# Three hand-written orders of one two-layer kernel, written anew

## The chip, the cores and the metric

One core of a Trainium2 chip runs the whole program. The metric is the device time of one execution in microseconds (us). It is measured on the chip, and several runs are taken. A profile of one execution comes with it: the start and duration of the instructions of each engine, what an engine waited for, and when the transfers landed. PE is the matrix engine, DVE the vector engine, ACT the scalar engine. POOL and SP issue transfers here and do little else.

## The reference

The input `x` is 16 images of 128 channels by 64 by 64 pixels, in float32. Two layers follow each other, both added to their input:

```python
# layer 0
v   = round(clip(gn(x) * input_factor, -1, 1) * 127) / 127 * 0.6     # group norm, then 8 bits
fv  = patches(v) + 0.1 * patches(v) ** 3                             # 3x3, padded by one
outs = [einsum('bctfyx,ocyx->btfo', fv, (g_pos - g_neg)[i]) for i in range(3)]
adc  = lambda y: clip(round(y * 0.01 * 256) / 256, -16, 16)
x = x + (adc(outs[2]) + 4*adc(outs[0]) + 2*adc(outs[1]) + 1*adc(outs[2])) * output_factor + bias
# layer 1
h  = gn(x)
q, k, v = Wq h, Wk h, Wv h
x  = x + Wm (q * (exp(B) (exp(k) * v)) / (exp(B) exp(k)))
```

`gn` is a group norm over 32 groups of 4 channels with all pixels of an image. So layer 0 is three 3x3 convolutions of 128 to 128 channels per image (one for each slice of the weights), and layer 1 is a chain of small matrix products for each pixel.

## The kernel before, in words

**The work.** A 3x3 convolution is done by a transform in both directions (rows by four, columns by two), so that it needs fewer products: an image's convolution with one weight slice (a *block*, 0, 1 or 2) has two halves, numbered `k` = 0 to 5 over the three blocks. Each product is 128x128 by 512 columns in float32. Layer 1 works on an image in four chunks, each a *pair* (numbers 0 to 3) of 1024 pixels.

**The operations.** Every step is a small function with a name, and three strings give the order in which the functions are called. The order in which they are called is the order of the instructions on every engine, because the schedule is manual. Each engine works through its own instructions strictly in this order; semaphores between engines are put in by the framework, where one operation needs another. Names that matter here:

- `q10.k q11.k q20.k ... q31.k`: PE, the products of half `k`, for two columns of the transform (last digit 0 or 1 before the dot). `q1u` starts a sum in a PSUM bank, `q2u` and `q0u` add to it, `q3u` adds to another bank.
- `m1u.k` (ACT, after `q1u`, before `q2u`), `sdu.k` (ACT, after `q2u`, before `q0u` and `q3u`), `sAu.k` (ACT, after `q0u`, before the next half's `q1u`): copies of the bank between the products. So PE needs ACT between any two of them.
- `Bo.k df.k sm.k` (DVE; `sm` of an even half is an adding transfer issued by POOL), `S0 S3 ma mc` (DVE): the back transform.
- `P.k`, `bc.k`, `o0.k o1.k`, `tk.k`: PE's product shared by two columns, DVE's spreading of it, eight more products of PE on the same bank, and ACT's taking of the bank. `bA bB` (DVE) bound the values, `aA aB` add them to the accumulator: for blocks 1 and 2 by an adding transfer on POOL's queue.
- `cx0..cx3` (ACT) turn the finished accumulator into four chunks; they need the last adding transfer `aB.1`. `cd0x..cd3x` (POOL) add the input to them by a transfer; `sq0..sq3` (ACT) sum squares; `ya pmy yb pvy yc yl yd` is the group norm between the layers (DVE, PE and ACT by turns).
- `xn kp vp qp ek ekv dn g u ln ex oa ob oc op r rd st` with a pair's number: layer 1. `xn ek g ln ex r` are ACT's, `kp vp qp dn op` PE's, `ekv u oa ob oc` DVE's, `rd` a transfer on POOL's queue and `st` a store on SP's.
- `li lj` (SP) load a chunk of the next image twice; `sx sy` (ACT) sum it and its squares, `x0 xa pmx xb pvx xc xl xd` is its group norm, `n` (ACT), `cl` (DVE), `s` (ACT), `va` (DVE) make the 8-bit values and their cubes, `gr er pa pb cs cq cd p0 p5 e0 e5` (DVE) the forward transform, `cp` (ACT) a copy.
- At the beginning only: `hs` (DVE, sum of a chunk), `hq` (ACT, its squares), `hn hc hr hv` as `n cl s va`, `hz hcs hcq hcd` (DVE, transform), and `W0a` to `W2p`: `Wia` negates weight slice `i` (ACT), `WiA` adds the positive weights to it by a transfer on POOL's queue, the other letters transform the weights (`c d e f h i k l o p` on DVE, `b g j J m n` on ACT).

**The lists.** `ORDER` is called for images 2 to 14 (13 times); an entry `q10.3+1` belongs to the turn before, so that the end of one image lies among the beginning of the next. `FIRST` is the work ahead of that: the weights and images 0 and 1. `LAST` is all that comes after, to the last store. Before the lists run, the four chunks of image 0 are loaded: 0 and 2 on SP's queue, 1 and 3 on ACT's. The lists are read by

```python
    for p in range(2, B - 1):
        turns[p] = operations(p)
        for e, s in order:
            o = turns[p - s].pop(e, None)
            if o is not None:
                o()
```

Of the kernel before, what the change touches and what calls it, by code (L numbers as in the profile page):

```python
# [70 lines left out]
    sA0.0+1 pmx+1 W2h+2 q31.0+1 q11.1+1 m11.1+1 xb+1 cq1+2 q10.1+1 W1l+2 m10.1+1 q21.1+1 lj1+1
    Bo.0+1 W2J+2 pvx+1 W2j+2 q20.1+1 sd0.1+1 q00.1+1 sd1.1+1 q01.1+1 W1k+2 q30.1+1 df.0+1 xc+1
    W1m+2 q31.1+1 p0+1 xl+1 W1o+2 W1n+2 xd+1 sA0.1+1 e0+1 n1+1 P.2+1 sm.0+1 q10.2+1 W1p+2 W2i+2
    Bo.1+1 W2l+2 n0+1 sA1.1+1 df.1+1 q11.2+1 m10.2+1 q20.2+1 sd0.2+1 cl0+1 q00.2+1 sm.1+1
    m11.2+1 ma.2+1 q21.2+1 sA0.2+1 sd1.2+1 q10.3+1 mc.2+1 q01.2+1 p5+1 s0+1 cl1+1 S0.2+1
    q30.2+1 q31.2+1 va0+1 s1+1 S3.2+1 sA1.2+1 lj3+1 W2m+2 q11.3+1 W2n+2 m10.3+1 Bo.2+1 bc.2+1
    m11.3+1 q20.3+1 bA.2+1 va1+1 df.2+1 q21.3+1 lj2+1 e5+1 sd0.3+1 sd1.3+1 n3+1 o1.2+1 n2+1
    o0.2+1 q00.3+1 gr0+1 q30.3+1 q31.3+1 sA0.3+1 q01.3+1 tk.2+1 P.3+1 W2p+2 li0+0 er0+1 sA1.3+1
    W2o+2 q10.4+1 Bo.3+1 sm.2+1 cp+1 bc.3+1 df.3+1 q11.4+1 m11.4+1 o0.3+1 cl2+1 cl3+1 W2k+2
    sx0+0 sm.3+1 s2+1 va2+1 mc.4+1 ma.4+1 q21.4+1 m10.4+1 q20.4+1 sd0.4+1 o1.3+1 sd1.4+1 S0.4+1  # L80
    aA.2+1 x0+0 q30.4+1 li1+0 tk.3+1 S3.4+1 q00.4+1 sA0.4+1 q31.4+1 P.4+1 bc.4+1 s3+1 q01.4+1
    q10.5+1 Bo.4+1 o1.4+1 bB.3+1 va3+1 sx1+0 bA.4+1 er1+1 m10.5+1 q20.5+1 sA1.4+1 aA.4+1 sy1+0
    q11.5+1 m11.5+1 o0.4+1 gr1+1 sd0.5+1 li3+0 tk.4+1 sy0+0 q21.5+1 P.5+1 q00.5+1 sd1.5+1
    q01.5+1 df.4+1 pb0+1 sA1.5+1 q30.5+1 sA0.5+1 q31.5+1 bc.5+1 pa0+1 o1.5+1 Bo.5+1 cq0+1
    df.5+1 cs0+1 o0.5+1 li2+0 tk.5+1 P.0+0 q10.0+0 sm.4+1 m10.0+0 q11.0+0 m11.0+0 sm.5+1
    q20.0+0 sd0.0+0 q21.0+0 sd1.0+0 cd0+1 q01.0+0 mc.0+0 aB.3+1 S0.0+0 bB.5+1 bc.0+0 sx2+0
    pa1+1 ma.0+0 pb1+1 q00.0+0 sA0.0+0 q30.0+0 o0.0+0 S3.0+0 o1.0+0 sy2+0 q31.0+0 aB.5+1 cs1+1
    sx3+0 sy3+0 bA.0+0 aA.0+0 tk.0+0 P.1+0 sA1.0+0 q11.1+0 q10.1+0 m10.1+0 lj1+0 bc.1+0 o0.1+0
# [9 lines left out]
    lj3+2 q31.2+2 S3.2+2 cl1+2 sA1.2+2 P.2+2 bc.2+2 q10.3+2 m10.3+2 q11.3+2 s1+2 cl0+2 Bo.2+2  # L98
    q20.3+2 bA.2+2 o0.2+2 m11.3+2 s0+2 sd0.3+2 sq1+2 va1+2 q21.3+2 sd1.3+2 lj2+2 o1.2+2 q30.3+2
    st3+2 sq2+2 q00.3+2 va0+2 sq3+2 q01.3+2 q31.3+2 df.2+2 gr0+2 tk.2+2 P.3+2 ya+2 pmy+2  # L100
    sA0.3+2 q10.4+2 er0+2 sA1.3+2 q11.4+2 yb+2 pvy+2 bc.3+2 Bo.3+2 n3+2 o1.3+2 cp+2 yc+2
    m10.4+2 n2+2 df.3+2 yl+2 st2+2 m11.4+2 yd+2 o0.3+2 xn0+2 cl2+2 cl3+2 sm.2+2 sm.3+2 mc.4+2
    s3+2 q20.4+2 kp0+2 vp0+2 ma.4+2 S0.4+2 tk.3+2 q21.4+2 P.4+2 sd0.4+2 q00.4+2 ek0+2 s2+2
    ekv0+2 dn0+2 sA0.4+2 va2+2 bB.3+2 sd1.4+2 g0+2 bc.4+2 u0+2 xn1+2 q10.5+2 oa0+2 q30.4+2
    o1.4+2 ln0+2 ex0+2 aA.2+2 o0.4+2 tk.4+2 q01.4+2 kp1+2 va3+2 qp0+2 ob0+2 bA.4+2 vp1+2 ek1+2
    gr1+2 oc0+2 op0+2 aB.3+2 q31.4+2 er1+2 sA1.4+2 ekv1+2 S3.4+2 Bo.4+2 q11.5+2 r0+2 P.5+2
    bc.5+2 dn1+2 df.4+2 pa0+2 m10.5+2 pb0+2 q20.5+2 m11.5+2 q21.5+2 sd0.5+2 g1+2 sd1.5+2 o1.5+2
    oa1+2 u1+2 o0.5+2 rd0+2 cs0+2 q00.5+2 ln1+2 ex1+2 sA0.5+2 tk.5+2 q30.5+2 cd0+2 q01.5+2
    q31.5+2 ob1+2 cq0+2 st0+2 bB.5+2 xn2+1 q10.0+1 qp1+2 oc1+2 sA1.5+2 kp2+1 vp2+1 m10.0+1
    ek2+1 op1+2 Bo.5+2 df.5+2 ekv2+1 q11.0+1 r1+2 m11.0+1 q20.0+1 aA.4+2 sm.5+2 dn2+1 sm.4+2  # L110
    mc.0+1 sd0.0+1 g2+1 S0.0+1 aB.5+2 q21.0+1 sd1.0+1 P.0+1 bc.0+1 u2+1 pa1+2 oa2+1 ln2+1 ex2+1
    ma.0+1 q00.0+1 rd1+2 q01.0+1 st1+2 ob2+1 S3.0+1 pb1+2 xn3+1 o1.0+1 o0.0+1 tk.0+1 q30.0+1
    kp3+1 qp2+1 vp3+1 oc2+1 op2+1 q31.0+1 cs1+2 ek3+1 ekv3+1 sA1.0+1 cq1+2 q11.1+1 Bo.0+1 r2+1
    P.1+1 bc.1+1 dn3+1 rd2+1 sA0.0+1 df.0+1 bA.0+1 g3+1 q10.1+1 sm.0+1 o0.1+1 u3+1 m10.1+1
    oa3+1 cd1+2 m11.1+1 o1.1+1 ln3+1 q21.1+1 tk.1+1 q20.1+1 bB.1+1 ex3+1 aA.0+1 sd0.1+1 sd1.1+1
    qp3+1 q00.1+1 sA0.1+1 ob3+1 oc3+1 q01.1+1 sA1.1+1 op3+1 r3+1 q10.2+1 aB.1+1 rd3+1 q30.1+1
    p0+1 m10.2+1 q31.1+1 e0+1 cx0+1 cd0x+1 q20.2+1 q11.2+1 cx1+1 cx2+1 p5+1 Bo.1+1 sd0.2+1
    P.2+1 df.1+1 y0+1 cd1x+1 m11.2+1 q21.2+1 sm.1+1 cd2x+1 cx3+1 mc.2+1 S0.2+1 sd1.2+1 q00.2+1
    q30.2+1 sA0.2+1 q01.2+1 ma.2+1 sA1.2+1 q10.3+1 bc.2+1 S3.2+1 e5+1 q11.3+1 q31.2+1 cd3x+1
    bA.2+1 o0.2+1 Bo.2+1 st2+1 st3+1 sq0+1 sq1+1 m10.3+1 m11.3+1 q20.3+1 df.2+1 sq2+1 q21.3+1  # L120
    sd0.3+1 sd1.3+1 o1.2+1 q30.3+1 sq3+1 q00.3+1 q31.3+1 ya+1 pmy+1 tk.2+1 P.3+1 yb+1 sA0.3+1
# [850 lines left out]
```

## Time and profile before

| What | us |
|---|---|
| median of 3 runs | 1596.8 (1596.6 to 1596.85) |
| span of the profiled execution, first to last instruction | 1594.6 |
| so outside the span, by the median | 2.2 |
| PE busy | 1488.2 |
| DVE busy | 1476.9 |
| ACT busy | 1184.6 |
| the first convolution product on PE | 46.6 |
| product `q10.3` in the first turn of ORDER, start | 156.74 |
| the same product in the 13th turn, start | 1287.74 |
| so one turn, the mean of the 12 between | 94.25 |

A line of the profile such as `L557 PE MATMUL` names the line of the kernel: L557 are all convolution products, L580, L582 and L585 ACT's copies `m1`, `sd` and `sA`, L588, L589 and L626 DVE's `Bo`, `df` and `bc`, L634 is `tk`, L644 `aB` and `aA`, L705 `cx`, L451 `n`, L365 all sums of squares, L434 `hs`, L318 the weights' `c`. One product of the convolution is two instructions, so `x2` on PE is one product. In a row of the timeline the first number is the start, the second the time covered, and what stands in brackets at the end is the idle time of the engine just before and what ended it.

### The profile page before, as it was taken

What the parts mean: (1) busy time and instruction counts of PE and PEld (TensorE: products, weight loads), DVE (VectorE), ACT (ScalarE), POOL (GpSimd) and SP (SyncE); (2) the same over time, 40 slices, a digit from 0 to 9 for tenths busy, and PEclk for the clock granted to TensorE, in tenths of its full rate; (3) what the DMA queues carried; (4) which work ended last, traced back from release to release, by engine and by line L of the source; (5) the groups of instructions that cost most, each with busy time, mean ns of one, the idle gap of its engine ahead of it and who ended that gap; (6) DMA issues with size and microseconds to landing.
All of it is one profiled execution on the core that took longest, in us unless ns stands there. A gap on an engine that the chain in (4) does not pass through costs nothing.

```text
span 1594.6 us, 14947 instructions
## 1 busy us (share of the span) xinstructions
PE 1488.2 (93%) x4684; PEld 564.8 (35%) x4684; DVE 1476.9 (93%) x1915; ACT 1184.6 (74%) x1859; POOL 227.8 (14%) x254
## 2 busy tenths in 40 slices
...
GB/s 184 81 92 119 104 160 173 124 206 111 148 130 166 184 119 191 125 136 144 149 208 115 154 130 151 163 134 197 117 149 133 157 183 119 202 62 123 76 128 149
DMA packets 67361, 227.03 MB, mean 142 GB/s; under 512 B 7632, under 2 KB 8272, under 8 KB 67280
## 3 DMA queue, kind: packets, MB, share of 16 engines
...
## 4 chain that ended last, share of the span: by engine, by line
PE 54%; issue 14%; DMA 13%; DVE 12%; ACT 5%; POOL 2%; DVEq 0%; POOLq 0%; ACTq 0%; SPq 0%
PE py L557 18%; PE pa L557 17%; PE pz L756 5%; PE pb L557 5%; DMA x<-in_x_dram 4%; PE pz L766 3%; DMA s<-s 3%; PE py L756 3%; DMA acc<-y 3%; PE py L778 2%; ACT x L705 2%; DVE acc L611 1%; DMA gmat<-in_x_dram 1%; DVE y L611 1%; DVE s L616 1%
## 5 line engine op out<-in xcount | busy, mean ns | idle before, releaser
L557 PE MATMUL py<-v,ud 128*128 128x512 f32 x760 | 357.5, 608 | 0.5
L557 PE MATMUL pa<-cs,us 128*128 128x512 f32 x384 | 199.2, 621 | 40.1 <-DVE cs L515 31.5
L557 PE MATMUL pa<-cd,us 128*128 128x512 f32 x384 | 202.8, 619 | 12.1 <-ACT pb L582 12.1
L557 PE MATMUL pa<-cq,us 128*128 128x512 f32 x384 | 198.5, 613 | 14.3 <-ACT d L580 14.2
L557 PEld LDWEIGHTS py<-v,ud 128*128 128x128 f32 x760 | 138.9, 189 | 182.0 <-issue 148.4
L557 PE MATMUL pb<-cd,us 128*128 128x512 f32 x384 | 194.3, 602 | 2.0 <-ACT pb L582 1.9
L580 ACT ACTIVATE d<-pa 128x512 f32<-128x512 f32 x192 | 112.1, 594 | 36.3 <-PE pa L557 20.4
L585 ACT ACTIVATE s<-pa 128x512 f32<-128x512 f32 x192 | 110.6, 591 | 35.3 <-PE pa L557 33.3
L582 ACT ACTIVATE pb<-pa 128x512 f32<-128x512 f32 x192 | 112.5, 586 | 29.7 <-PE pa L557 29.0
L819 POOL DMA_DIRECT2D xn<-x x58 | 58.3, 1010 | 521.1 <-ACT xn L789 520.8
L644 POOL DMA_DIRECT2D acc<-y x62 | 68.8, 1109 | 392.2 <-DVE y L637 243.7
L588 DVE SCALAR_TENSOR_TENSOR s<-d,pb 128x1024 f32<-128x1024 f32 x96 | 116.9, 1218 | 2.4 <-PE pb L557 2.0
L756 PE MATMUL pz<-xn,w 128*64 128x512 f32 x464 | 117.7, 607 | 0.6 <-ACT xn L803 0.6
L589 DVE TENSOR_TENSOR d<-s 128x1024 f32<-128x1024 f32 x96 | 117.3, 1221 | 0.4
L557 PEld LDWEIGHTS pa<-cs,us 128*128 128x128 f32 x384 | 66.0, 191 | 137.7 <-issue 64.4
L634 ACT ACTIVATE y<-py 128x1024 int16<-128x1024 f32 x62 | 82.6, 1333 | 41.4 <-PE py L557 40.2
L789 ACT ACTIVATE xn<-py,scalars 128x512 f32<-128x512 f32 x116 | 73.5, 685 | 51.1 <-PE py L778 51.1
L557 PEld LDWEIGHTS pa<-cq,us 128*128 128x128 f32 x384 | 68.0, 190 | 121.6 <-issue 71.9
L557 PEld LDWEIGHTS pa<-cd,us 128*128 128x128 f32 x384 | 66.8, 190 | 125.0 <-ACT pb L582 57.1
L557 PEld LDWEIGHTS pb<-cd,us 128*128 128x128 f32 x384 | 70.3, 190 | 96.4 <-issue 85.6
L557 PE MATMUL py<-sv,ud 128*128 128x512 f32 x192 | 98.6, 596 | 4.0 <-ACT y L634 1.9
L597 POOL DMA_DIRECT2D s<-s x48 | 45.3, 945 | 332.8 <-ACT gs L365 119.8
...
## 6 DMA issues: line engine op xcount, KB each, us to landing
xc<-in_x_dram SPq DMA_DIRECT2D x121, 512.0 KB, 5.4
...
```

The costliest lines, as they stand in the source:

```text
L557: pe.matmul(o if len(r.shape) == 2 else o.rearrange("p (t w) -> p t w", w=W2), w, r, start=start, stop=stop, skip_group_check=True,)
L580: f"m1{u}.{k}": lambda u=u, a=a: act.activation(d[:, u], a, AF.Copy),
L582: f"sd{u}.{k}": lambda a=a, b=b: act.activation(b, a, AF.Copy, scale=-1.0),
L585: f"sA{u}.{k}": lambda u=u, a=a: act.activation(s[:, u, 0], a, AF.Copy),
L588: f"Bo.{k}": lambda: dve.scalar_tensor_tensor(s[:, :, 1], d, 2.0, pb, ALU.mult, ALU.add),
L589: f"df.{k}": lambda: dve.tensor_tensor(d, s[:, 1], s[:, 0], ALU.subtract),
L634: act.activation(self.column(self.part(1)[0], h), y, AF.Copy)
L644: pool.dma_start(a, y, accum_op=ALU.add)
L756: pe.matmul(self.tiles(o)[h * IC : (h + 1) * IC], w, x[:, t[0] : t[1] : t[2]], start=True, stop=True)
L766: pe.matmul(o[c, t], eb[r, c], self.half(x)[r, t], start=True, stop=True, skip_group_check=True)
L789: act.activation(g[:, t], self.tiles(self.op[h]), AF.Identity, bias=bias_sb)
L819: "rd": lambda: pool.dma_start(self.r, self.x2, accum_op=ALU.add),
```

## The change

The three strings are replaced. No function differs, and every operation is called as often as before, for the same images. In `ORDER` each of the 307 entries is there again; six of them change the turn that they are counted to, since the cut between two turns lies elsewhere by a few entries (`P.2 q31.2 sA1.2` now on one side, `cd3x q30.2 sq0` on the other). `FIRST` has the same 409 entries and `LAST` the same 570, but for those six. The whole of `ORDER`, the beginning of `FIRST`, and the last image's end in `LAST`:

```diff
 ORDER = """
-    S3.2+1 cl1+1 q31.2+1 q10.3+1 cl0+1 P.2+1 sA1.2+1 q11.3+1 m10.3+1 bc.2+1 q20.3+1 o1.2+1 s1+1
-    m11.3+1 s0+1 Bo.2+1 sd0.3+1 sq1+1 va1+1 lj3+1 q21.3+1 o0.2+1 va0+1 sd1.3+1 q30.3+1 sq2+1
-    q00.3+1 q01.3+1 tk.2+1 lj2+1 sq3+1 df.2+1 er0+1 sA1.3+1 gr0+1 sA0.3+1 n3+1 P.3+1 ya+1 q31.3+1
-    bc.3+1 pmy+1 yb+1 n2+1 q11.4+1 st2+1 sm.2+1 q10.4+1 pvy+1 m10.4+1 o1.3+1 o0.3+1 Bo.3+1 yc+1
-    m11.4+1 df.3+1 yl+1 cp+1 yd+1 xn0+1 tk.3+1 ma.4+1 sm.3+1 q20.4+1 cl3+1 kp0+1 vp0+1 ek0+1
-    q21.4+1 mc.4+1 st3+1 cl2+1 sd0.4+1 bA.2+1 s3+1 S0.4+1 P.4+1 li0 xn1+1 s2+1 sd1.4+1 ekv0+1
-    bc.4+1 va3+1 q00.4+1 va2+1 dn0+1 g0+1 o0.4+1 o1.4+1 li1 q01.4+1 u0+1 ln0+1 oa0+1 tk.4+1 q30.4+1
-    S3.4+1 kp1+1 gr1+1 qp0+1 vp1+1 ex0+1 sA0.4+1 sx0 sA1.4+1 ob0+1 q31.4+1 bA.4+1 sx1 oc0+1 ek1+1
-    op0+1 er1+1 aA.2+1 q11.5+1 r0+1 q10.5+1 Bo.4+1 ekv1+1 m11.5+1 P.5+1 pa0+1 q21.5+1 x0 bc.5+1
-    pb0+1 m10.5+1 dn1+1 q20.5+1 rd0+1 g1+1 sy1 o1.5+1 o0.5+1 st0+1 sd0.5+1 u1+1 oa1+1 cs0+1 df.4+1
-    ln1+1 sd1.5+1 q00.5+1 ex1+1 tk.5+1 ob1+1 q30.5+1 cd0+1 qp1+1 q01.5+1 q31.5+1 sy0 xn2 oc1+1
-    cq0+1 sA1.5+1 Bo.5+1 op1+1 kp2 sA0.5+1 bB.3+1 vp2 aA.4+1 q10.0 q11.0 df.5+1 r1+1 li3 bB.5+1 ek2
-    m10.0 P.0 aB.3+1 sm.5+1 ekv2 sm.4+1 m11.0 q20.0 q21.0 rd1+1 dn2 mc.0 S0.0 sd0.0 sd1.0 q00.0
-    bc.0 li2 g2 q30.0 sx3 aB.5+1 u2 oa2 pb1+1 o1.0 o0.0 ln2 pa1+1 sA0.0 ex2 sx2 q31.0 tk.0 q01.0
-    ob2 st1+1 xn3 ma.0 qp2 kp3 oc2 op2 cs1+1 sy3 r2 vp3 S3.0 ek3 bA.0 sA1.0 q10.1 sy2 P.1 Bo.0
-    q11.1 ekv3 m10.1 bc.1 dn3 cq1+1 aA.0 g3 o0.1 u3 o1.1 cd1+1 ln3 oa3 lj1 q20.1 ex3 m11.1 tk.1 ob3
-    rd2 q21.1 qp3 lj0 bB.1 sd0.1 sd1.1 xa aB.1 q00.1 oc3 op3 q01.1 sA0.1 p0 r3 q10.2 sA1.1 e0 pmx
-    df.0 p5 q30.1 rd3 q31.1 m10.2 cx0 e5 xb pvx sm.0 cx1 q11.2 y0 Bo.1 q20.2 cx2 xc m11.2 xl q21.2
-    sd0.2 cd0x df.1 q00.2 cx3 sm.1 xd sd1.2 cd2x mc.2 q01.2 cd1x ma.2 S0.2 n1 cd3x sA0.2 n0 sq0
-    q30.2
+    S3.2+1 cl0+1 bc.2+1 q30.2+1 q11.3+1 cl1+1 q10.3+1 sq2+1 cd3x+1 m11.3+1 q21.3+1 Bo.2+1 s0+1
+    m10.3+1 s1+1 o0.2+1 sq0+1 q20.3+1 va0+1 sd1.3+1 sd0.3+1 va1+1 o1.2+1 df.2+1 sq1+1 q31.3+1 tk.2+1
+    bA.2+1 gr0+1 q00.3+1 sq3+1 ya+1 q01.3+1 lj3+1 P.3+1 q30.3+1 bc.3+1 lj2+1 st2+1 sA1.3+1 pmy+1
+    yb+1 sA0.3+1 er0+1 q10.4+1 n3+1 m10.4+1 q11.4+1 cl3+1 n2+1 pvy+1 yc+1 sm.2+1 m11.4+1 o1.3+1
+    Bo.3+1 yl+1 yd+1 o0.3+1 q20.4+1 df.3+1 xn0+1 kp0+1 tk.3+1 vp0+1 li0 P.4+1 sm.3+1 cl2+1 mc.4+1
+    S0.4+1 ek0+1 cp+1 q21.4+1 sx0 sd0.4+1 ekv0+1 dn0+1 s2+1 sd1.4+1 bc.4+1 g0+1 st3+1 o1.4+1 s3+1
+    ma.4+1 o0.4+1 u0+1 va2+1 q00.4+1 oa0+1 ln0+1 q30.4+1 x0 ex0+1 va3+1 tk.4+1 ob0+1 q01.4+1 qp0+1
+    li1 xn1+1 vp1+1 gr1+1 oc0+1 sA0.4+1 kp1+1 S3.4+1 op0+1 er1+1 sA1.4+1 ek1+1 q11.5+1 r0+1 q31.4+1
+    m11.5+1 ekv1+1 q10.5+1 pa0+1 sx1 P.5+1 m10.5+1 rd0+1 dn1+1 Bo.4+1 q20.5+1 sy1 bc.5+1 li3 o0.5+1
+    pb0+1 g1+1 bA.4+1 q21.5+1 o1.5+1 sy0 sd1.5+1 u1+1 cs0+1 ln1+1 sd0.5+1 ex1+1 q31.5+1 cd0+1 tk.5+1
+    st0+1 xn2 q00.5+1 aA.2+1 oa1+1 df.4+1 q01.5+1 ob1+1 sA0.5+1 sA1.5+1 qp1+1 q30.5+1 bB.5+1 li2
+    oc1+1 sx3 Bo.5+1 q10.0 cq0+1 m10.0 bB.3+1 op1+1 r1+1 vp2 sx2 kp2 aA.4+1 ek2 df.5+1 q11.0 sm.5+1
+    sm.4+1 rd1+1 q20.0 sd0.0 ekv2 sy3 P.0 sy2 m11.0 aB.3+1 dn2 mc.0 g2 q00.0 aB.5+1 q30.0 sA0.0
+    q21.0 S0.0 bc.0 u2 o1.0 pa1+1 ma.0 o0.0 sd1.0 st1+1 oa2 q31.0 ln2 q01.0 ex2 tk.0 xn3 sA1.0 lj1
+    qp2 pb1+1 ob2 kp3 cs1+1 oc2 op2 r2 ek3 vp3 Bo.0 bA.0 q10.1 S3.0 ekv3 P.1 lj0 cq1+1 rd2 dn3 bc.1
+    q11.1 g3 m11.1 u3 xa df.0 oa3 cd1+1 o0.1 o1.1 m10.1 q20.1 ln3 tk.1 ex3 bB.1 sd0.1 q21.1 pmx ob3
+    qp3 xb aA.0 sd1.1 sm.0 oc3 q00.1 aB.1 op3 sA0.1 pvx p5 q10.2 q01.1 p0 r3 m10.2 xc xl xd e5 sA1.1
+    q31.1 q30.1 cx2 Bo.1 rd3 cd2x q11.2 cx0 cd0x e0 cx1 q20.2 df.1 m11.2 sd0.2 q21.2 cx3 cd1x y0
+    q00.2 sm.1 mc.2 S0.2 sd1.2 q01.2 ma.2 n0 P.2 n1 sA1.2 sA0.2 q31.2
 """
 FIRST = """
-    hs0+2 x0+2 hq0+2 hs1+2 hq1+2 hq2+2 hq3+2 W0a+2 W0A+2 hs2+2 hs3+2 xa+2 W1a+2 pmx+2 xb+2
-    pvx+2 W2a+2 xc+2 xl+2 hi+2 xd+2 W0b+2 W0c+2 hn1+2 hn0+2 W0e+2 W2A+2 hc0+2 hc1+2 W0d+2 W0f+2
-    hn3+2 W2f+2 li0+1 hc3+2 hr1+2 hv1+2 hr0+2 hv0+2 li1+1 W2c+2 W0j+2 er0+2 hn2+2 W0g+2 W1A+2
...
+    hs2+2 hs0+2 hs1+2 hs3+2 x0+2 hq3+2 hq2+2 hi+2 hq0+2 hq1+2 ho+2 xa+2 pmx+2 xb+2 pvx+2 xc+2 xl+2
+    xd+2 hn1+2 hn0+2 W0a+2 W2a+2 hn3+2 hc1+2 hc0+2 hr1+2 hv1+2 W0A+2 hr0+2 hn2+2 hc2+2 hc3+2 li0+1
...
 LAST = """
...
-    tP1+0 tp0+0 Lx1+0 oc3+0 sm.5+1 tma+0 op3+0 Lc3+0 Lx3+0 r3+0 tmc+0 tb1+0 tp1+0 tP0+0 tS1+0
-    tb2+0 tS0+0 rd3+0 tx1+0 tk3+0 tsh+0 ts1+0 to0+0 tx2+0 ts2+0 to1+0 tk0+0 tb3+0 tb0+0 tx0+0
-    ts0+0 tx3+0 ts3+0 st3+0 tna+0 tpm+0 tnb+0 tpv+0 tnc+0 tnl+0 tnd+0 Xn0+0 Xn2+0 Xn1+0 Kp0+0
...
+    df.5+1 tP1+0 sm.5+1 Lx2+0 Lc1+0 oc3+0 tma+0 tmc+0 tp0+0 tS1+0 tb1+0 op3+0 tp1+0 tS0+0 r3+0 Lx1+0
+    tP0+0 tk3+0 to0+0 rd2+0 rd3+0 tb2+0 tb3+0 tx1+0 tx2+0 to1+0 tsh+0 ts1+0 ts2+0 st2+0 tk0+0 tx3+0
+    tb0+0 ts3+0 tx0+0 ts0+0 tna+0 tpm+0 rd1+1 tnb+0 tpv+0 tnc+0 tnl+0 tnd+0 Xn0+0 Xn1+0 Kp0+0 Ek0+0
...
 """
```

The new `FIRST` goes on with `hv0 W1a gr0 er0 cp hr2 W0c W0b W0e hr3 W0j sx0 W0d`. In the last image's end, `Lc` and `Lx` are that image's `cx` and `cd`, `tx` and `ts` its sums and sums of squares, and `tk3` takes a bank (DVE).

133 lines of the change are left out of this document (65 added, 68 removed).

## The prediction

> **What bounds the kernel now.** I read the page first: its span and its busy shares.
>
> ```profile
> span 1594.6 us, 14947 instructions
> PE 1488.2 (93%) x4684; PEld 564.8 (35%) x4684; DVE 1476.9 (93%) x1915; ACT 1184.6 (74%) x1859; POOL 227.8 (14%) x254
> ```
>
> Two engines are nearly full. No operation is added or removed, so only idle time can be won or lost. The busy time by stage tells whose idle time counts (columns: stretch and length, then busy PE, PEld, DVE, ACT, POOL, granted clock, DMA):
>
> ```profile
> 40.00:80.00 40.00, 28.56 (x59) 10.91 (x59) 39.72 (x58) 25.13 (x47) 0.84 (x1) 0.85 0.27 80
> 120.00:156.00 36.00, 31.42 (x71) 12.60 (x70) 33.69 (x44) 23.15 (x39) 7.57 (x8) 0.95 0.56 112
> 156.00:1381.00 1225.00, 1196.82 (x3798) 453.03 (x3797) 1171.13 (x1507) 955.14 (x1496) 181.13 (x195) 1.00 0.64 150
> ```
>
> Up to 156 us (FIRST) DVE sets the pace: it is full from 40 to 120, PE is not. In the 13 turns of ORDER (156 to 1381) PE leads, with 28.2 us idle, 2.2 a turn. But DVE has only 53.9 us idle, 4.1 a turn: 90.1 of 94.25 are busy. So the head is read on DVE and the loop on PE.
>
> **The head: what the new FIRST costs.** DVE's timeline from the start:
>
> ```profile
> 5.88 1.22 DVE L434 TENSOR_REDUCE x<-xc 128x1 f32<-128x1024 f32 x1 [3.73 <-DMA xc<-in_x_dram]
> 10.57 2.35 DVE L434 TENSOR_REDUCE x<-gmat 128x1 f32<-128x1024 f32 x2 [2.16 <-DMA gmat<-in_x_dram]
> 13.18 0.16 DVE L369 TENSOR_REDUCE x<-x 128x2 f32<-128x8 f32 x1 [0.26 <-ACT gs L365]
> 20.23 0.56 DVE L318 TENSOR_TENSOR s<-s 128x384 f32<-128x384 f32 x1 [3.01 <-DMA s<-in_g_pos_dram]
> ```
>
> Chunks 0 and 1 are there at 5.9, chunk 2 at 10.57. Before, `hs0` and `x0` run at once and ACT squares two chunks meanwhile, so `xa` starts at 13.18. `xd` ends at 17.2, and then DVE loses 3.0 us, since `W0c`, queued ahead of `hn1`, waits for the positive weights.
>
> The new list puts `hs2` first. DVE then stands until 10.57, does four sums at 1.17 (2.35 for two) until 15.25, and only then `x0`. Four squares on ACT, 1.28 apart (10.63 to 11.91), follow: `xa` at 20.4, 7.2 later. `xa` to `xd` took 4.0; three weight negations that stood before `xl` on ACT are gone from there, so 3.5: `xd` ends at 23.9, where `hn1` started at 20.7 before. Next, ACT has `hn0` 1.2, `W0a` 1.06, `W2a` 1.17, `hn3` 1.2, `hr1` 1.0, and DVE's fourth step `hv1` waits for the last of them, until 29.6: 4.0 idle after 25.6. `hc2` waits for `hn2` (1.0 idle). `W0e` waits for `W0b`, queued behind `cp` and `hr2` (1.5 idle). From there I find nothing that DVE waits for.
>
> Until the first product, before: 46.4 us, of which 33.4 are DVE work by the list, 13.0 idle. After: 10.57 + 4.9 (for the squares) + 1.3 (in the norm) + 0.2 + 4.0 + 1.0 + 1.5 = 23.5 idle. That is **+10.5**, the first product at about 58. The DVE work ahead of later marks is the same in both lists to 1 us (image 0's `q10.2` 53.7 and 53.1, `q11.3` 66.6 and 66.0), so the list does not give it back. DVE idles 2.3 us between 120 and 156, which can swallow part. I take **+10**, with 6 (that, and half of the wait for `hv1`) and 12 as ends.
>
> **The loop: what the new ORDER wins.** One boundary between two turns, in the timelines of PE, ACT and POOL:
>
> ```profile
> 515.10 1.88 PE L557 MATMUL pa<-cq,us 128*128 128x512 f32 x4
> 526.78 1.12 PE L557 MATMUL pa<-cq,us 128*128 128x512 f32 x2 [0.35 <-ACT d L580]
> 529.23 1.12 PE L557 MATMUL pa<-cd,us 128*128 128x512 f32 x2 [0.47 <-ACT pb L582]
> 534.55 1.13 PE L557 MATMUL pa<-cs,us 128*128 128x512 f32 x2 [0.76 <-ACT s L585]
> 539.54 1.02 PE L557 MATMUL py<-v,ud 128*128 128x512 f32 x2
> ```
> ```profile
> 515.30 1.32 ACT L634 ACTIVATE y<-py 128x1024 int16<-128x1024 f32 x1 [0.46 <-PE py L557]
> 522.74 1.15 ACT L705 ACTIVATE x<-acc,scalars 128x1024 f32<-128x1024 int16 x1
> 526.15 0.57 ACT L580 ACTIVATE d<-pa 128x512 f32<-128x512 f32 x1
> 528.60 0.57 ACT L582 ACTIVATE pb<-pa 128x512 f32<-128x512 f32 x1
> ```
> ```profile
> 517.64 1.19 POOL L644 DMA_DIRECT2D acc<-y  x1 [7.14 <-DVE x L371]
> ```
>
> *A chain that stays.* `o1.1` ends at 515.1, `tk.1` (515.30), `bB.1`, `aB.1` issued at 517.64 and landed 5.0 later, three `cx` (from 522.74), `m11.2` (526.15), `sd0.2`, `cx3`, `sd1.2` (528.60), and PE's `q01.2` at 529.23: 14.1 us. The new list has the same chain, with the same PE products from `o1.1` to `q01.2`. It takes `xl` (0.33) out from between `m11.2` and `sd0.2`, but `xl` and `sA1.1` now stand ahead of the first `cx`, which starts some 0.3 later. I put it at nothing, ends -0.3 and +0.5; PE's waits before `m11.2` and `sd1.2` change places only.
>
> *Stalls behind it that go.* From `q01.2` (529.23) to the end of `o0.2` (539.54 and 1.76) is 12.1 us for eight products and two groups of four. PE waits for `sA1.2`, which stands on ACT behind `n0` and `sq0` (row 534.55), and the next two each come 0.25 late. Now ACT has `sd1.2 n0 n1 sA1.2`: 3.0 us, while PE has four products, 3.6, before `q11.3` needs it; `bc.2` gets 2 products more of room. The ten then take 8 times 0.9 and 2 times 1.78, 10.8: **-1.3** a turn, ends 0 and -1.5.
>
> *A detour less.* A change between convolution and layer-1 products costs PE about 0.1 each way, as around `op3` here: 1.06 from one start to the next instead of 0.86, and 0.96 for the product after.
>
> ```profile
> 517.92 1.12 PE L557 MATMUL pa<-cd,us 128*128 128x512 f32 x2
> 518.98 1.13 PE L778 MATMUL py<-ekv,wm 64*128 64x512 f32 x4
> 520.04 1.12 PE L557 MATMUL pa<-cd,us 128*128 128x512 f32 x2
> 521.00 1.02 PE L557 MATMUL pa<-cs,us 128*128 128x512 f32 x2
> ```
>
> `kp1 qp0 vp1`, then `q31.4`, then `op0` becomes `qp0 vp1 kp1 op0`: **-0.2**.
>
> *New tight places.* `cq1` (1.15) moves ahead of `bc.1` on DVE: from `qp2`'s end, `oc2 Bo.0 bA.0 S3.0 ekv3 cq1 bc.1` need 6.45 and PE reaches `o0.1` after 6.75. Next `u3 xa df.0 oa3 cd1 bB.1 ob3 xb oc3` need 7.65 against 7.45 on PE before `op3`: **+0.1**, ends 0 and +1. `sy3 sy2` stand before `m11.0` on ACT (3.5 us against 3.8 on PE): 0.
>
> Sum of a turn: -1.3 - 0.2 + 0.1 = -1.4; 13 turns, **-18**, ends 0 (DVE, at 90.1 of 94.25, gives no more) and -28.
>
> *Moved transfers.* `sm.0` goes ahead of `aB.1` and `rd3` on POOL's queue, `df.0` earlier, so `mc.2` no longer waits for it (1.28 idle on DVE here, not on PE's path). `aB.1` is issued some 3.5 us after it; an adding transfer lands 5 to 6.5 after its issue, so they overlap a little. Best nothing, worst +2.6 a turn (two transfers in a row); I take 0, being nearer to the row of 5.0. `li2` now stands behind `st0` on SP, and `xn2` waits for `st0`: 4.6 for `rd0` and 4.9 for `st0` from `r0`'s end give 0.9 us of room. 0.
>
> *The clock.* After an idle time of 2.64 us PE ran slowly for 3.6 us (the clock of 0.95 in the stretch to 156):
>
> ```profile
> 151.65 3.53 PE L557 MATMUL pa<-cd,us 128*128 128x512 f32 x4 [2.64 <-ACT pb L582]
> ```
>
> I expect 1.15 before `m11.2`, and 1.5 more in the two turns or so where `aB.1` lands late (a wait of 1.79 at 811.64 shows one): 2.65, where this row was. By the row that costs 1.7 in such a turn, 0 to 3.4 in all; I take 0, since 2.14 at 716.34 did nothing. [...]
>
> **The end.** On DVE `tx1` waits 1.32 (1549.21) for the last chunk's input. Now `tk3`, 1.18 long, fills that wait and `tx0` is last: **-1**, ends -4 and +4 for the last two images' boundaries, which I did not follow entry by entry.
>
> **Sum.** 1594.6 + 10 - 18 - 1 = 1585.6; the median lies 2.2 above the span: **1587.8**.
>
> **The rivals.**
> - *DVE takes over in the loop (slower).* Place: `qp2` to `op3`, where DVE has 14.1 us of work for 14.2 of PE. If each turn loses 0.8 there or at a like place, the loop wins 0.6 a turn, 8 in all, and head and end leave +1; at 0.3 a turn, 1602. It decides as soon as a turn wins less than 0.7. For it: 4.1 us of idle DVE in a turn are all there is, and strict queues can use no more than part. Against it: several of its waits are for PE, and shrink as PE does. 1596 to 1608.
> - *The transfer turn (slower).* `aB.1` lands behind `sm.0`: up to +34, 1610 to 1622. Against: 3.5 us between their issues.
> - *The head costs little.* If DVE's loss is made up by 156: +3, so 1581; with the full 2 us a turn won, 1573. Against: DVE is full from 40 to 120.
> - *It does less than it says* cannot be: the entries are the same.
>
> **How the numbers follow.** Forecast, 1576 to 1594: 0.54. DVE's rival 0.30, of which 0.08 falls within the bound. Transfers 0.06. Cheap head 0.10. A measurement of this kernel tells 0.2% (3.2 us) from no change. Of the forecast 0.04 lies within it. Faster 0.50 + 0.10 = 0.60; same 0.04 + 0.08 = 0.12; slower 0.22 + 0.06 = 0.28. Range 1572 to 1608: it leaves out the transfer case, the worst of the DVE case and a little below.
>
> **What would show it.** First product at 56 to 60. `hs2` first on DVE, idle until 10.6. `q10.3` to `q10.3` 92.4 to 93.3. No wait before `q11.3`; one of about 1.2 before `q21.2`. `mc.2` without a wait for a transfer. Wrong would be: a first product before 52, a turn above 93.6, or a landing of `aB.1` over 6 us in most turns.

## The result, and the profile after

The new lists take **1635.2 us** (median of 4, 1631.5 to 1636.2) against 1596.8 for the old ones in the same comparison: ratio 1.0241, 95% interval 1.0227 to 1.0256. The forecast was 1587.8 with a range to 1608, so the sign was wrong too. The page of the profiled execution after:

```profile
span 1633.7 us, 14888 instructions
PE 1493.5 (91%) x4684; PEld 569.2 (35%) x4684; DVE 1482.3 (91%) x1915; ACT 1174.3 (72%) x1859; POOL 225.0 (14%) x254
```

The span grew by 39.1 us, the busy time of PE and DVE by 5 each: most of what came is waiting. The stretches that were shown of before, after the change (same columns):

```profile
40.00:80.00 40.00, 18.61 (x39) 7.21 (x40) 39.62 (x60) 25.58 (x63) 0.84 (x1) 0.72 0.23 66
120.00:156.00 36.00, 32.09 (x73) 12.78 (x71) 33.80 (x37) 16.30 (x26) 3.84 (x5) 1.00 0.40 88
156.00:1381.00 1225.00, 1172.45 (x3692) 449.05 (x3692) 1150.17 (x1475) 928.14 (x1466) 173.74 (x190) 0.99 0.63 146
```

In the long stretch PE did 3692 instructions where it did 3798: the loop itself is slower. To split the 39.1 I use one small product that both lists have once per image, `pmy`, in PE's timeline. Before, for images 1 and 14:

```profile
168.95 0.28 PE L384 MATMUL pz<-y,grp 128*128 128x1 f32 x2
1396.78 0.28 PE L384 MATMUL pz<-y,grp 128*128 128x1 f32 x2
```

and after (its line number is 5 smaller, since the lists are 5 lines shorter):

```profile
183.57 0.28 PE L379 MATMUL pz<-y,grp 128*128 128x1 f32 x2
1439.31 0.28 PE L379 MATMUL pz<-y,grp 128*128 128x1 f32 x2
```

So the head costs +14.6, the 13 turns between the marks cost 1255.7 - 1227.8 = +27.9 (2.1 a turn), and the rest wins 3.4. Together 39.1.

What the loop waits for is in PE's list of waits, from 172 to 1381 us (columns: line, who was waited for, sum, times, longest). Before, its three largest rows:

```profile
PE pa L557 <- ACT d L580: 9.2, 13, 2.1
PE pa L557 <- ACT s L585: 6.6, 9, 1.0
PE pa L557 <- ACT pb L582: 6.1, 13, 0.5
```

After, the two largest:

```profile
PE pz L751 <- ACT ek L802: 22.2, 12, 1.9
PE pa L552 <- ACT d L575: 16.9, 13, 2.2
```

The waits for `s` (`sA1.2`) and `pb` (`sd`) that the forecast wanted to see go are gone. A wait that before did not have at all is there in every turn: 1.85 us ahead of a projection into `pz`, until an `ek` has run. Its place in PE's and in ACT's timeline:

```profile
622.95 1.13 PE L773 MATMUL py<-ekv,wm 64*128 64x512 f32 x4
625.94 1.08 PE L751 MATMUL pz<-xn,w 128*64 128x512 f32 x4 [1.85 <-ACT ek L802]
```
```profile
624.13 1.27 ACT L784 ACTIVATE xn<-py,scalars 128x512 f32<-128x512 f32 x2 [1.82 <-PE py L773]
625.29 0.60 ACT L802 ACTIVATE ek<-pz 128x512 f32<-128x512 f32 x1
```

These are `op2`, then `r2` and `ek3` on ACT, then `vp3`. The new `ORDER` reads `op2 r2 ek3 vp3`; the old one had `op2 .. r2 vp3 S3.0 ek3`. `ek3` reads the first half of the tile `pz`, `vp3` writes the second half: no value passes between them. But in the trace after, `vp3`'s first product waits 1.85 us until `ek3` has run (625.94), and in that of before it waits for nothing (`vp3` at 506.68, with no idle time ahead of it).

### The profile page after: what moved, and what is told of

The parts are those of the page before. It is cut to its first block, busy times and chain, and to the rows that moved or that the text cites. A ratio compares the mean times of both kernels' runs of the same rounds, so it can differ in the third digit from the quotient of the medians.

```text
span 1633.7 us, 14888 instructions
## 1 busy us (share of the span) xinstructions
PE 1493.5 (91%) x4684; PEld 569.2 (35%) x4684; DVE 1482.3 (91%) x1915; ACT 1174.3 (72%) x1859; POOL 225.0 (14%) x254
## 3 DMA queue, kind: packets, MB, share of 16 engines
q1 hardware_dynamic: 28512, 99.50, 17.7%
## 5 line engine op out<-in xcount | busy, mean ns | idle before, releaser
L552 PE MATMUL pa<-cs,us 128*128 128x512 f32 x384 | 204.8, 629 | 36.9 <-DVE cs L510 35.5
L552 PE MATMUL pa<-cd,us 128*128 128x512 f32 x384 | 198.4, 613 | 7.5 <-ACT pb L577 5.7
L575 ACT ACTIVATE d<-pa 128x512 f32<-128x512 f32 x192 | 112.1, 592 | 42.7 <-PE pa L552 37.7
L814 POOL DMA_DIRECT2D xn<-x x58 | 51.3, 884 | 634.8 <-ACT xn L784 634.8
L580 ACT ACTIVATE s<-pa 128x512 f32<-128x512 f32 x192 | 107.3, 591 | 31.3 <-PE pa L552 30.9
L552 PE MATMUL py<-sv,ud 128*128 128x512 f32 x192 | 102.4, 617 | 1.8 <-ACT y L629 1.1
L777 ACT ACTIVATE gs<-pz,scalars 128x512 int32<-128x512 int32 x60 | 40.9, 682 | 72.8 <-PE pz L761 67.0
## 6 DMA issues: line engine op xcount, KB each, us to landing
x<-in_g_neg_dram SPq DMA_DIRECT2D x2, 576.0 KB, 11.3
```

Source lines behind the costliest of these rows:

```text
L552: pe.matmul(o if len(r.shape) == 2 else o.rearrange("p (t w) -> p t w", w=W2), w, r, start=start, stop=stop, skip_group_check=True,)
L575: f"m1{u}.{k}": lambda u=u, a=a: act.activation(d[:, u], a, AF.Copy),
L580: f"sA{u}.{k}": lambda u=u, a=a: act.activation(s[:, u, 0], a, AF.Copy),
L777: act.activation(self.half(self.g).bitcast(I32), self.den.bitcast(I32), AF.Identity, bias=magic, scale=-1.0)
L814: "rd": lambda: pool.dma_start(self.r, self.x2, accum_op=ALU.add),
```

## The experiments

Numbers are those of the labels; there is no twelfth. All times are medians, and "before" in the same comparisons was 1595.7 to 1597.9.

**1. `ek3` behind `vp3`.** One entry of the new `ORDER`:

```diff
- op2 r2 ek3 vp3 Bo.0
+ op2 r2 vp3 ek3 Bo.0
```


> The changed kernel with one entry of ORDER moved: ek3 stands behind vp3 instead of ahead of it; FIRST and LAST are those of the change. Theory: in the new ORDER the second projection of pair 3 (vp3, into the second half of pz) waits until ek3 has read the first half, and PE stands 1.85 to 1.92 us in each of the 13 turns (row 625.94 of the profile after). Then this kernel takes 25 us less than the changed one, 1608 to 1612, its turn is 94.4 to 94.7 us instead of 96.44, and PE has no wait ahead of vp3. Rival, the one on record: DVE paces the turn, and a wait taken off PE comes back as another wait of PE for DVE: then a gain of 0 to 10 us, 1625 to 1635, and a turn above 95.7.

1605.2 us, 30 less than the change; ratio to before 1.0055 (1.0040 to 1.0070). PE's waits in the same stretch:

```profile
PE pa L552 <- ACT d L575: 17.7, 12, 3.1
PE py L552 <- DVE py L621: 2.7, 13, 0.3
```

The row for `ek` is gone, and between the two `pmy` marks a turn is 94.2 us (after 96.6, before 94.4). The stretch between the marks as a whole, after the change and in this experiment:

```profile
183.57:1439.31 1255.74, 1202.12 (x3797) 459.39 (x3796) 1176.60 (x1509) 946.42 (x1496) 178.41 (x195) 0.99 0.63 147
```
```profile
183.47:1407.55 1224.08, 1195.15 (x3797) 457.12 (x3796) 1175.32 (x1509) 946.12 (x1496) 178.31 (x195) 1.00 0.65 151
```

It is 31.7 us shorter. 24.7 of that is idle time of PE, the 25 of the theory. The other 7.0 is PE's busy time for the same number of instructions: after the change the granted clock was 0.50 for 3.41 us at five places between the marks, here at one (see the last section).

**2. The same, the other way round**, in the kernel before:

```diff
- op2 cs1+1 sy3 r2 vp3 S3.0 ek3
+ op2 cs1+1 sy3 r2 ek3 vp3 S3.0
```


> The kernel before with one entry of ORDER moved: ek3 directly behind r2 and so ahead of vp3. Theory: the order of ek3 and vp3 alone makes the wait. On ACT ek3 runs at 507.95 to 508.55 in the profile before in either case, and vp3 started on PE at 506.68; it would now start at 508.5. So 1.9 us a turn, 25 us, 1619 to 1624. Rival: what is lost at vp3 is won back at the turn's other waits of PE (0.9 ahead of q21.2, 0.6 ahead of q01.2 and q11.3), so less than 12 us, 1597 to 1609.

1628.0 us, ratio 1.0204 (1.0185 to 1.0223): 32 more, from one entry moved by two places, and above the 1619 to 1624 of the theory. The row that comes is the same as after the change, to the digit:

```profile
PE pz L751 <- ACT ek L802: 22.2, 12, 1.9
```

And the whole stretch between the marks, before and in this experiment:

```profile
168.95:1396.78 1227.83, 1197.84 (x3798) 452.85 (x3797) 1173.29 (x1509) 955.29 (x1496) 181.14 (x195) 1.00 0.64 150
```
```profile
169.17:1430.56 1261.39, 1206.78 (x3796) 456.14 (x3797) 1177.01 (x1509) 956.71 (x1497) 181.05 (x195) 0.99 0.63 147
```

PE idles 24.6 us longer, as the theory has it, and is busy 8.9 longer: no place at half clock between the marks before, five here. So the order of these two entries makes the wait, nothing absorbs it, and some of the waits bring half clock with them. Whether two tiles in place of one `pz` would free `vp3` was not tried.

**3. The old `FIRST` under the new `ORDER`** (seam made to fit, see the expectation).

> The changed kernel with the list FIRST of before (three entries that the new ORDER expects to be done, P.2 q31.2 sA1.2, added at its end, and three that it still does, cd3x q30.2 sq0, taken off). Theory: the new FIRST costs what the two profiles show when image 1 is under way (pmy of the second image at 169.0 and 183.6), 14.6 us, and nothing of it is given back later: 1619 to 1623. Rival: what is lost after the first product (3.3 of the 14.6) belongs to the phase in which the loop is entered and not to FIRST: then 1623 to 1626. If the loop gave back a part of the head, it would be less than 10: 1625 or more.

1623.4 us, 11.8 less than the change. But the seam made a wait of its own, on ACT and so on PE (two views):

```profile
164.74 1.15 ACT L360 ACTIVATE gs<-x,y 128x1024 int16<-128x1024 f32 x1 [5.72 <-DMA x<-in_x_dram]
```
```profile
166.52 2.07 PE L552 MATMUL pa<-cq,us 128*128 128x512 f32 x2 [5.46 <-ACT d L575]
```

The new `ORDER` squares chunk 2 first (`sq2`), and the old `FIRST` loads it last. So this run does not price `FIRST` by itself: its `pmy` of image 1 comes at 177.81, 5.8 earlier than after the change, and the loop between the marks is 8.75 shorter, with one place at half clock in place of five. Experiment 10 mends the seam; there that `pmy` comes 15.9 earlier than in 9 (168.82 for 184.67), near the 14.6.

**4. The new `LAST` under the old `ORDER`.**

> The kernel before with the list LAST of the change (three entries made to fit at its start). Theory: the new LAST is worth the 4.4 us by which the distance between the two profiles shrinks from pair 3 of the turn before the last (43.5) to the end (39.1), most of it where the kernel before waits 3.43 us ahead of m11.2 and q21.2 of the last image: 1591 to 1594. Rival: the gain belongs to the way in which the new ORDER leads into LAST; then nothing, 1596 to 1598.

1595.7, ratio 0.9999 (0.9989 to 1.0008): nothing. The theory fell: the 3.4 us that the end won belong to the way in which the two lists meet.

**5. The old opening in the new `FIRST`.**

```diff
- hs2+2 hs0+2 hs1+2 hs3+2 x0+2 hq3+2 hq2+2 hi+2 hq0+2 hq1+2 ho+2
+ hs0+2 x0+2 hq0+2 hs1+2 hq1+2 hq2+2 hq3+2 hs2+2 hs3+2 hi+2 ho+2
```


> The changed kernel with only the first eleven entries of FIRST in the order of before (hs0 x0 hq0 hs1 hq1 hq2 hq3 hs2 hs3 hi ho). Theory: of the 11.3 us by which the first product is late, 7.2 are hs2 and the four sums ahead of x0; xa starts at 13.2 again, the first product at about 50.7, and the time falls by 7 (5 to 9): 1626 to 1630. Rival: what is won at the opening is lost again behind it (DVE waits for hn3, hr1 and the weights whatever the opening), so at most 3 us: 1632 to 1635.

1627.9, 7.3 less than the change. PE's first product, and image 1's `pmy`, are 7.4 earlier than after the change:

```profile
50.54 3.75 PE L552 MATMUL pa<-cs,us 128*128 128x512 f32 x4 [35.54 <-DVE cs L510]
...
176.15 0.28 PE L379 MATMUL pz<-y,grp 128*128 128x1 f32 x2
```

**6. `m11.2` ahead of a chunk.** PE's largest wait that remains in the loop is the one for `d` (`m11.2`), behind three `cx` on ACT.

```diff
- cx0 cd0x e0 cx1 q20.2 df.1 m11.2 sd0.2 q21.2 cx3 cd1x y0 q00.2 sm.1 mc.2 S0.2 sd1.2 q01.2
+ cx0 cd0x e0 q20.2 df.1 m11.2 sd0.2 cx1 q21.2 cd1x y0 q00.2 sm.1 mc.2 S0.2 sd1.2 cx3 q01.2
```


> The kernel of the first experiment (ek3 behind vp3) with two entries of ORDER moved: cx1 from ahead of m11.2 to behind sd0.2, and cx3 from ahead of sd1.2 to behind it. Theory: PE's wait ahead of q21.2 (1.12 to 1.29 us a turn) is for m11.2, which stands on ACT behind three cx of 1.13 us, though its product q11.2 is done by 539.7 and the third cx starts at 540.09; with m11.2 there PE goes on 1.1 us earlier, a turn is 93.0 to 93.4 us, and the time 12 to 14 us under the 1605.2 of that experiment: 1591 to 1594. Rival, the one on record: DVE has no more to give; or sq3, which waits for a chunk that the later cx3 lets start 0.55 later, holds ACT up: a gain of at most 5, 1600 to 1605.

1622.8, 17.5 more instead of 13 less. The wait ahead of `q21.2` is gone, and the mistake is that of the change itself in another place: `cx3` went behind `mc.2`, which writes the accumulator that `cx3` reads, so it waits for it (and a quarter of the fourth chunk is then the next image's, in this kernel and the next two). DVE, ACT and PE:

```profile
547.99 1.36 DVE L606 SCALAR_TENSOR_TENSOR acc<-s,s 128x1024 int16<-128x1024 f32 x1
```
```profile
549.39 1.15 ACT L700 ACTIVATE x<-acc,scalars 128x1024 f32<-128x1024 int16 x1 [1.91 <-DVE acc L606]
```
```profile
553.59 3.53 PE L552 MATMUL pa<-cs,us 128*128 128x512 f32 x4 [2.37 <-ACT s L580]
```

**7 and 8. More parts on that kernel.** 7 takes the old `FIRST` and, in `LAST`, puts `ek1` and `ek0` behind `vp1` and `vp0`; 8 changes 7 in `FIRST`:

```diff
- xd+2 W0b+2 W0c+2 hn1+2 hn0+2 W0e+2 W2A+2 hc0+2 hc1+2 W0d+2
+ xd+2 hn1+2 hn0+2 hc0+2 hc1+2 W0b+2 W0c+2 W0e+2 W2A+2 W0d+2
```


> The kernel of the experiment before this one, with the FIRST of before, and in LAST the two entries ek1 and ek0 that stood ahead of vp1 and vp0 put behind them (PE waited 0.76 and 0.84 us for them). Theory: the parts add up: 12 us for FIRST, as the third experiment had it, and 1.5 for LAST, off that kernel: 1577 to 1581, under both kernels. Rival: if that kernel's own gain falls out, 1589 to 1593.

> The kernel of the experiment before this one with hn1 hn0 hc0 hc1 moved ahead of W0b W0c W0e W2A in FIRST. Theory: in the profile before, DVE loses 3.01 us because W0c waits for the positive weights (20.23) with hn1 (1.0) and hc0 hc1 (0.77) queued behind it; moved ahead, 1.8 us of DVE's work falls into that wait, and the head is 1.8 shorter: 1575 to 1579, 1 to 2 under the kernel it is made from. Rival: DVE then waits for hn3 or hr1 on ACT by as much: no difference.

1613.7 (9 under 6, with a seam wait of 3.35 inside) and 1614.6: the fill of DVE's 3 us gained nothing. Its wait for the positive weights was 0.93 now, but a second one of 1.49 for the other slice followed, and the first product came at 46.9 (46.8 in 7). The rival of 8 had the outcome right; DVE's new wait is for weights, though, and not for ACT.

**9. The order of 6 mended**: `m11.2 sd0.2 cx1 q21.2 sd1.2 cx3`, ahead of `mc.2`.

> The kernel of the sixth experiment, with sd1.2 and cx3 moved up so that cx3 stands ahead of mc.2 again: m11.2 sd0.2 cx1 q21.2 sd1.2 cx3. In the sixth the PE's wait ahead of q21.2 was gone, but cx3 stood behind mc.2 of the next image in the list, ACT waited 1.91 us for mc.2 and sA1.2, queued behind, came late (553.59, 2.37 us on PE). Theory: that order was all that was wrong with it, and the wait ahead of q21.2 is worth what it lasts: 0.7 to 1.1 us a turn, 1591 to 1597, 8 to 14 under the first experiment (1605.2). Rival, the one on record: DVE, where mc.2 now waits 0.45 us longer for cx3, gives nothing: 1602 to 1607.

1606.0: no gain over experiment 1. The wait ahead of `q21.2` is gone and two others stand in its place on PE, for `sA1.2` and for `m11.3`; on DVE `mc.2` waits for `cx3`:

```profile
548.52 1.98 PE L552 MATMUL pa<-cs,us 128*128 128x512 f32 x4 [0.82 <-ACT s L580]
551.04 1.13 PE L552 MATMUL pa<-cq,us 128*128 128x512 f32 x2 [0.53 <-ACT d L575]
```
```profile
545.14 1.39 DVE L606 SCALAR_TENSOR_TENSOR acc<-s,s 128x1024 int16<-128x1024 f32 x1 [0.76 <-ACT x L700]
```

`sA1.2` overwrites what `S0.2` reads, `m11.3` what `S3.2` reads; both come on DVE behind `mc.2`.

**10. All together**, 9 with the old `FIRST` (chunk 2 first at its end) and the mended `LAST`.

> The kernel of the experiment before this one, with the FIRST of before, in whose last entries chunk 2 is read and loaded ahead of chunks 0 and 1 (as the new ORDER squares it first; in the third experiment PE lost 5.5 us at the seam, where sq2 waited for that chunk), and with ek1 and ek0 of LAST behind vp1 and vp0. Theory: FIRST is worth 12 to 15, LAST 1.5: 1576 to 1583, under both kernels. Rival: the seam or the loop takes it back: 1585 to 1597.

1591.7, ratio 0.9972 (0.9961 to 0.9984): under both kernels, 14.3 under 9, as the parts said, but short of the range, by what 9 did not bring.

**11. The same idea in the kernel before**: `cx2` behind `sd0.2`, `cx3` behind `sd1.2`.

> The kernel before with cx2 moved behind sd0.2 and cx3 behind sd1.2 (both still ahead of mc.2). Theory: its stalls ahead of q21.2 and q01.2 (0.35 and 0.47 at 526.78 and 529.23) are also m11.2, sd0.2 and sd1.2 behind the cx on ACT; without them the turn is 0.4 to 0.7 us shorter: 1588 to 1592. Rival: P.2 and sA1.2, which follow and wait as well, wait longer instead, since cx3 and n1 come later on ACT: 1594 to 1598.

1597.8, ratio 1.0009 (0.9999 to 1.0019). Nothing; the rival.

**13. Without the transfer `aB.1`**, on experiment 1: the call of `aB` does nothing for `k` = 1.

> The kernel of the first experiment (ek3 behind vp3) without the adding transfer aB.1; half of the third block's result is missing from the output. Theory, formed after the ninth and eleventh experiments, in which a wait taken off PE came back as another: the wait of PE at a turn's boundary is set by one chain through three engines, from the landing of aB.1 through the four cx (537.83 to 543.34 in the first experiment) and on DVE through mc.2, S0.2, ma.2 and S3.2 to m11.3 and q21.3 (548.74 and 549.38). The cx then needn't wait 5 us for the landing, PE's waits at the boundary go (1.5 us a turn over the shortest step, and the late landings), and the turn is 92.4 to 92.9 us: 1584 to 1591, 14 to 21 under the first experiment (1605.2). Rival, the one on record: DVE's own work paces the turn, and PE's waits go elsewhere: 1599 to 1606.

1605.6, as experiment 1. The landing does not set the turn: the quickest turns take 93.3 us between two `pmy`, 93.5 in experiment 1. ACT's queue was busy until the first `cx` anyway. That the totals are equal is in part chance, though. In this profile one turn took 99.4: another adding transfer landed 9.2 us after its issue, `tk`, which overwrites what it reads, waited on ACT, and PE waited for `tk`:

```profile
800.98 1.30 ACT L629 ACTIVATE y<-py 128x1024 int16<-128x1024 f32 x1 [5.64 <-DMA acc<-y]
```
```profile
802.34 1.08 PE L751 MATMUL py<-xn,w 128*64 128x512 f32 x4 [3.36 <-ACT y L629]
```

The other twelve turns take 93.7 on the mean, the same twelve of experiment 1 94.2. So late landings of `aB.1` may cost up to 0.4 a turn, 5 us; one profile of each does not settle it, and the 14 to 21 of the theory are far.

**14 to 17. Other queues relieved.** These missed what they aimed at. 14, 16 and 17 moved `r3` and its transfer `rd3` behind `cx3`, which overwrites the chunk that `rd3` reads (that pair's residual is then taken from another image), and the chunks' loads queued behind it: 1707.1, 1708.5 and 1707.4, all three only a measure of that. 15 moved `e5`, which stands ahead of `Bo.1` where DVE waits anyway: 1606.2, nothing.

> The kernel of the run before (no adding transfer aB.1; half of the third block's result is missing) with r3 and rd3 moved behind sd1.2, so that the cx stand 1.27 us earlier in ACT's queue. Theory: at the boundary three chains end together at mc.2 (543.14 in the run before): the landing, ACT's queue (r3 m10.2 xl sA1.1 and four cx without a gap from 534.86 to 542.95), and DVE's (Bo.1 e5 df.1 y0 sm.1, 539.05 to 543.0, behind a product of PE). Taking two away leaves the third: no gain, 1602 to 1606, PE's wait ahead of q21.2 gone and one ahead of q11.3 or q21.3 in its place. Rival: ACT alone paced the boundary: 12 to 15 less, 1590 to 1594.

> No aB.1, r3 where it was, and e5 (0.6 us of DVE between Bo.1 and mc.2, needed only by P.3) moved behind df.2. Theory of the three chains: mc.2 can then start at 542.5 by DVE but at 542.95 by the fourth cx on ACT: 0.1 to 0.2 us a turn, 1601 to 1605. Rival: DVE alone paced it: 0.6 us a turn, 8 less, 1596 to 1599.

> No aB.1, r3 and rd3 behind sd1.2, and e5 behind df.2. Theory of the three chains: all three are shorter, mc.2 starts 0.6 us earlier or more, and the turn is 0.5 to 0.7 us shorter: 1594 to 1600. Rival: the turn is paced elsewhere (DVE's total of 90 us of work in 93.3): nothing, 1602 to 1606.

> As the run before, but with aB.1: the whole computation. Theory of the three chains: the landing (issue at 532.56 and 5.0 us) alone holds the first cx at 537.5, as ACT's queue did, so the fourth cx ends where it did and mc.2 starts where it did: 0 to 0.2 us a turn, 1602 to 1606, like the first experiment (1605.2). Rival: the landing is not among the chains, and the time is that of the run before.

**18. The boundary relieved in three places at once**, on experiment 1: no `aB.1`, no `r3`, and

```diff
- cx2 Bo.1 rd3 cd2x q11.2 cx0 cd0x e0 cx1
+ cx2 e0 Bo.1 rd3 cd2x q11.2 cx0 cd0x cx1
```


> The last three kernels didn't relieve what they were to relieve: with r3 behind cx3 the transfer rd3 reads chunk 3 after cx3 has overwritten it and the chunks' loads queue behind it, and e5 stands ahead of Bo.1, not behind it; e0 stands there. This kernel: that of the first experiment without aB.1 and without r3 (half of the third block's result and one pair's residual are missing), and with e0 ahead of Bo.1, where DVE waits 0.61 us for PE. Theory of the three chains: the landing is gone, ACT's queue ahead of the first cx is 1.27 us shorter, DVE's behind Bo.1 is 0.6 us shorter; mc.2 starts 0.6 us earlier, the turn is 0.5 to 0.7 us shorter than without aB.1 alone (1605.6): 1596 to 1600. Rival: the pace is DVE's total, and nothing at a boundary counts: 1602 to 1607.

1603.4, ratio 1.0040 (1.0028 to 1.0052): 2 us where 6 to 10 were expected. One turn of its profile took 98.8, as in 13. The first `cx` starts no earlier (72.1 to 72.4 us behind a turn's `pmy` in the turns without mishap, as in experiment 1), though neither the landing nor `r3` is ahead of it. PE's, DVE's and ACT's timelines show what is:

```profile
536.36 1.10 PE L552 MATMUL pa<-cs,us 128*128 128x512 f32 x2
```
```profile
537.63 0.22 DVE L395 SCALAR_TENSOR_TENSOR x<-x 128x1 f32<-128x1 f32 x1
```
```profile
537.50 0.60 ACT L575 ACTIVATE d<-pa 128x512 f32<-128x512 f32 x1 [1.76 <-PE pa L552]
538.00 0.19 ACT L398 ACTIVATE x<-x 128x1 f32<-128x1 f32 x1
538.22 0.20 ACT L399 ACTIVATE x<-x 128x1 f32<-128x1 f32 x1
538.36 0.60 ACT L580 ACTIVATE s<-pa 128x512 f32<-128x512 f32 x1
538.85 1.14 ACT L700 ACTIVATE x<-acc,scalars 128x1024 f32<-128x1024 int16 x1
```

ACT stands 1.76 us until PE has done `q10.2` (536.36), and then `m10.2` (L575), `xl` (L398 and L399) and `sA1.1` (L580) come ahead of the first `cx` (L700). `xc` on DVE (L395) ends at 537.85, before `xl` starts, so DVE holds `xl` up by little or nothing. What the `cx` wait for here is PE itself, which reaches `q10.2` without a wait. So the three chains that I had named were not the whole; the theory fell.

**19. The best version**: the whole computation, `FIRST` and `LAST` of 10, `ORDER` of 1, `e0` ahead of `Bo.1`.

> The whole computation: FIRST and LAST of the tenth experiment, the ORDER of the first (cx1 and cx3 where the change had them), and e0 ahead of Bo.1. Theory: as the ninth experiment was no faster than the first, the loop is that of the tenth to 0.1 us a turn, and e0 alone gains no more than 0.15 us a turn since mc.2 then waits for the fourth cx: 1588 to 1592, under both kernels like the tenth (1591.7). Rival: DVE alone paces the boundary: 0.6 us a turn, 1582 to 1585.

1587.4, ratio 0.9950 (0.9937 to 0.9962): under both kernels, and 4 under 10, a little more than the theory allowed. It differs from 10 in two things, `e0` and the places of `cx1` and `cx3`; what each gave was not separated. A clean turn of it (stretch, busy PE, PEld, DVE, ACT, POOL, clock, DMA):

```profile
437.80:531.10 93.30, 91.66 (x294) 35.17 (x292) 90.39 (x117) 72.81 (x116) 13.72 (x15) 1.00 0.66 152
```

and one of 18:

```profile
454.40:547.70 93.30, 91.65 (x294) 35.17 (x293) 90.40 (x117) 71.53 (x114) 12.48 (x14) 1.00 0.63 147
```

93.3 to 93.5 us is the turn without mishap in experiments 1, 13, 18 and 19, whatever was relieved. DVE works 90.4 of it.

## Why the prediction was wrong, point by point

- *What bounds it.* Right as far as it went: PE leads the loop with 2 us a turn idle, DVE follows closely.
- *The head: mechanism right, size short.* Step by step the opening came as written: `hs2` first at 10.33, `xa` at 20.12 (20.4), 3.78 of idle until `hv1` at 29.65 (29.6), waits of 0.97 and 1.46 (1.0 and 1.5), first product at 57.94 (58):

```profile
10.33 1.22 DVE L429 TENSOR_REDUCE x<-gmat 128x1 f32<-128x1024 f32 x1 [8.18 <-DMA gmat<-in_x_dram]
20.12 0.16 DVE L364 TENSOR_REDUCE x<-x 128x2 f32<-128x8 f32 x1 [5.01 <-ACT gs L360]
29.65 1.26 DVE L471 SCALAR_TENSOR_TENSOR f<-f,n 128x1056 f32<-128x1056 f32 x1 [3.78 <-ACT f L465]
```

  The first product is 11.3 later (57.94 for 46.61; 10.5 by the list). The mis-sized term is what follows. I let DVE's slack swallow a part and took 10, at most 12; it became 14.6. From the first product to image 1's `pmy` DVE was idle 6.1 us after, 3.0 before: while image 0's halves run, PE and ACT now wait for each other for 0.7 at a time, and DVE for them. "From there I find nothing that DVE waits for" was a reading of DVE's queue alone. Experiment 5 puts 7.3 on the opening.
- *The loop: the step that failed.* -18 was forecast, +27.9 came. The sum of a turn lacks a term: `vp3`'s wait for `ek3`, 1.85 of idle PE in each of the 13 turns, 24.1 in all. With the slower clock that it brought, the term is +2.4 a turn (96.6 for 94.2). I followed DVE through the very place (from `qp2`'s end to `bc.1`) and never asked, for each PE entry, which reader of its tile now stands ahead of it. "No operation is added or removed, so only idle time can be won or lost" misled twice: the order of the entries is what the waits are made from, and busy time moved too, PE's by +4.3 over before between the marks. Experiments 1 and 2 show it from both sides.
- *The -1.4 itself.* Without the missing term the loop is 94.2 against 94.4 a turn: -0.3, not -1.4. The stalls named did go (the rows for `s` and `pb`, 12.7 us in the stretch), and 1.12 ahead of `q21.2` is what the step on the chain said (1.15). But the row for `d` grew from 9.2 to 17.7, and small waits for DVE came. PE's idle time between the marks is 30.0 before and 28.9 in experiment 1, so the stalls' -1.3 a turn came back nearly whole as other waits; most of the -0.3 is PE's busy time (1197.8 and 1195.2). I ended the chain at `q01.2`. In experiment 9, which takes the wait ahead of `q21.2` off, it is seen to go on through `mc.2 S0.2 ma.2 S3.2` on DVE to `m11.3`. Experiments 9 and 11 took single waits off and won nothing.
- *The rivals.* "DVE takes over in the loop" had the right sign but not the cause. It reckoned with a loop that wins 0.3 a turn, and that is what experiment 1 wins once `ek3` is out of the way. That a clean turn stays at 93.3 with DVE at 90.4 speaks for it, but no run took work off DVE, so which chain makes the 93.3 stays open. The transfers' rival is refuted as the cause: adding transfers to the accumulator land in 5.2 us by the median, 5.7 before, `mc.2` waits for none, and without `aB.1` (experiment 13) at most 5 us can be read. "The head costs little" is refuted.
- *The end.* -3.4 against -1, inside its bounds; experiment 4 shows that `LAST` alone does not make it.
- *The clock.* Taken at 0, at most 3.4. For the loop that was reckoned with this is right: one place at half clock between the marks in experiment 1, none in 10 and 19. In the loop that came there are five, four of them behind the wait of 1.85, shorter than the 2.65 that I had reckoned with; PE's busy time is 7.0 above that of experiment 1, some 1.7 for each of the four more.
- *What would show it.* First product, `hs2`, the wait ahead of `q21.2`, none ahead of `q11.3`, no wait of `mc.2` for a transfer: all as written. Only the turn, 96.6 for 92.4 to 93.3, said that the sum was wrong.
